# A hybrid block on one core: the last batch's output projection is moved ahead of two other lanes' last products, and its norm reads the bank

## Chip, core and metric

The kernel runs on one core of one Trainium2 chip. The metric is the device time of one execution in microseconds (us), the median of several runs. Engines are named as the profile names them: PE (TensorE matmul), PEld (its weight load), DVE (VectorE), ACT (ScalarE), POOL (GpSimd), SP (the queue that issues most transfers).

## The reference, cut to what matters

Four sublayers, each a residual around a norm without learned factors, on `x` of 4 x 1024 x 128:

```python
x = x + attention(layernorm(x))      # 16 heads, sliding window and stride
x = x + ffn(layernorm(x))
x = x + mamba(layernorm(x))
x = x + ffn(layernorm(x))

def ffn(x):                          # weights are +1 or -1
    h = s0 * conn_dense(k0, concatenate([x, -x]))     # 128 -> 512
    h = s1 * conn_dense(k1, relu(h) * 2)              # 512 -> 512
    return s2 * conn_dense(k2, relu(h) * 2)           # 512 -> 128

def mamba(x):                        # adds its input once more itself
    ...                              # a scan over 1024 steps, 256 channels, 16 states
    y = (scan + u2 * D) * silu(z)
    return x + res_scale * (y @ W_out)
```

The change concerns the very end: the product with `W_out` of the second half of the last batch (512 rows), the norm after it and the MLP (`ffn`) that follows.

## The kernel before, in words

Attention comes first, then a setup of weights, then a long stage in which the scan sets the pace and everything else is slipped between its steps. A "unit" of the scan is one state of one half (512 steps) of one batch: 128 units in all, each with two scans on DVE (`hs`, two halves of 128 channels), one product on DVE (`hc`), one on POOL (`db`), folds on POOL (`hc` pairs) and sums on PE into the bank `pys` (loop at lines 1112 to 1139). When the last state of a part is summed, `gated` (line 1093) multiplies `gate` by `pys` on DVE, once for each half of the channels, and records that the gate is there.

The other work is written as generators that yield a `Piece` before each step (line 598): the engine time it should take, how many PSUM banks it needs, whether it empties a bank. A `Work` (line 625) wraps one generator. While the scan runs, `evictions` and `pieces` (lines 1155 and 1165) issue the next steps of the works in the order of the list `works`, with three banks among them (`SPARE`, line 1142). In this stage the program order on each engine is kept as written (`keep`, line 1240). After the last unit a loop (line 1251) issues, in the order of `works`, whatever is still open, and then the pools of that stage close.

What is still open then belongs to two lanes of MLP work. `pfoc` is the last MLP product of batch 2's second half (512 columns, 16 calls, which appear as 32 PE instructions), `pfob` the second half of the last MLP product of a tile of both batches (16 PE instructions). Each is followed by a residual on DVE (`ox` and `x`) and stores on SP.

Only then, with eight new banks, `mamba_out_own(B - 1)` runs (line 1256, through `weave`, line 640): for each of four groups of 128 rows two calls with the gate and `w_out` and two with an identity that adds the input `xs`; 32 PE instructions into the bank `pmo_own`. ACT copies the bank to `own_x` (`ox`, line 1041). Then the scan's buffers are released (`work.close()`), and two lanes of `late_batch` (line 784) run woven together, each on two of the four groups. Each calls `mlp` (line 682), which

- takes the norm's statistics with `ln_stats` (line 181): `bn_stats` and `bn_aggr` on DVE from `ox`, then four instructions on POOL per lane (add epsilon, power of -1/2, negate the mean, multiply), giving `rs_fc`;
- normalises on ACT, one instruction per group (`fxnc<-ox,rs_fc`);
- transposes on PE (`ftpc`), copies on ACT and subtracts on DVE to get a rounded part and a remainder (`fxnTc`);
- multiplies with the first weights (`pfc`, 16 PE instructions for both lanes), takes rounded part and remainder again on ACT and DVE (`h1c`), multiplies with the second weights (`pgc`, 64), takes the Relu on ACT (`h2c`), multiplies with the third (`pfoc`, 32) and adds the residual on DVE (`ox`), which a store of SP follows.

The trace gives one line, L57, to all compute instructions, that of the helper through which they are issued; they are told apart by tile.

Of the kernel before, what the change touches and what calls it, by code (L numbers as in the profile page):

```python
# [16 lines left out]
F32 = mybir.dt.float32  # L17
# [5 lines left out]
ALU = mybir.AluOpType  # L23
# [3 lines left out]
P = 128  # L27
B, T, C = 4, 1024, 128
# [7 lines left out]
EPS = 1e-5  # L36
# [7 lines left out]
def hybrid_kernel(ctx: ExitStack, tc: tile.TileContext, x, Wq, Wk, Wv, Wo, ln_g, ln_b, W_in, conv_w,  # L44
# [17 lines left out]
    ve, te, sc, gp = (InOrder(e) for e in (nc.vector, nc.tensor, nc.scalar, nc.gpsimd))  # L62
# [118 lines left out]
    def ln_stats(src, name, soon):  # L181

        n = src.shape[1]
        mv = yield from ln_sums(src, name, soon)
        yield Piece(gp=1.7)
        rs = small.tile([P, 2, n], F32, tag="rs", name=f"rs_{name}")
        gp.tensor_scalar_add(rs[:, 0], mv[:, :, 1], EPS)
        gp.tensor_tensor(rs[:, 0], rs[:, 0], minus_half[:, :n], ALU.pow)
        gp.tensor_scalar_mul(rs[:, 1], mv[:, :, 0], -1.0)
        gp.tensor_mul(rs[:, 1], rs[:, 1], rs[:, 0])  # L190
        yield Piece()
        return rs
# [429 lines left out]
    def evict(lump=False, **us):  # L622
        return Piece(evict=True, lump=lump, **us)
# [16 lines left out]
    def weave(*works):  # L640

        while any(w.next for w in works):
            for w in works:
                if w.may():
                    w.run()
# [33 lines left out]

    h1_free = [True]  # L680

    def mlp(u, tiles, split, pool, lane, own=None, soon=False, hasty=False):

        nt = tiles.shape[1]
        cols = nt * C
        parts = 2 if split else 1
        kind = F32R if split else F32

        def wt(w):
            return w if split else w.bitcast(F32)

        def empty(dsts, srcs, relu):


            n = len(srcs)
            yield Piece(n if split else 0, evict=True, sc=0.6 * n, same=soon or hasty)
            for dst, bk in zip(dsts, srcs):
                if relu:  # L700
                    sc.activation(dst[:, 0], bk, AF.Relu)
                else:
                    sc.copy(dst[:, 0], bk)
            if split:
                yield evict(ve=0.7 * n)
                for dst, bk in zip(dsts, srcs):
                    high = dst[:, 0].bitcast(F32)
                    if relu:
                        ve.scalar_tensor_tensor(dst[:, 1], bk, 0.0, high, ALU.max, ALU.subtract)
                    else:  # L710
                        ve.tensor_sub(dst[:, 1], bk, high)

        stats = yield from ln_stats(tiles, f"f{u}", soon)
        yield Piece(sc=1.7)
        xn = fx.tile([P, nt, C], F32, name=f"fxn{u}", tag=f"fxn{lane}", bufs=1)
        ln_apply(xn, tiles, stats[:, 0], stats[:, 1])
        yield fill(1.2)
        tp = bank(f"ftp{u}")[:, :cols]
        for i in range(nt):
            te.transpose(tp[:, i * P : (i + 1) * P], xn[:, i, :], ident)  # L720
        xnT = pool.tile([P, 2, cols], kind, name=f"fxnT{u}", tag=f"fxnT{lane}")
        yield from empty([xnT], [tp], False)
        for f0 in (0, 2):
            yield fill(1.0 if split else 1.8, 2, ready=(lambda: own or h1_free[0]) if f0 == 0 else None)
            if f0 == 0:
                if own:
                    h1 = own(u)
                else:
                    h1 = pool.tile([P, 4, 2, cols], kind, name=f"h1{u}", tag="h1")
                    h1 = [h1[:, f] for f in range(4)]  # L730
                    h1_free[0] = False
                h2 = pool.tile([P, 4, cols], F32, name=f"h2{u}", tag=f"h2{lane}")
            pf = [bank(f"pf{u}_{f0 + f}")[:, :cols] for f in range(2)]
            for f in range(2):
                w = wt(w0[:, (f0 + f) * P : (f0 + f + 1) * P])
                for s in range(parts):
                    te.matmul(pf[f], w, xnT[:, s], start=s == 0, stop=s == parts - 1)
            yield from empty(h1[f0 : f0 + 2], pf, True)
        for f0 in (0, 2):
            yield fill(2.0 if split else 1.8, 2)  # L740
            pg = [bank(f"pg{u}_{f0 + f}")[:, :cols] for f in range(2)]
            for f in range(2):
                for i in range(4):
                    if (i == 0 and f) or (i == 2 and not split):
                        yield more(2.0 if split else 1.8)
                    w = wt(w1[:, i, (f0 + f) * P : (f0 + f + 1) * P])
                    for s in range(parts):
                        te.matmul(pg[f], w, h1[i][:, s], start=i + s == 0, stop=i == 3 and s == parts - 1)
            yield evict(sc=1.2)
            for f in range(2):  # L750
                sc.activation(h2[:, f0 + f], pg[f], AF.Relu)
        if not own:
            h1_free[0] = True
        for i in range(nt):
            if i == 0:
                yield fill(2.0)
                po = bank(f"pfo{u}")[:, :cols]
            elif i == 2:
                yield more(2.0)
            for f in range(4):  # L760
                te.matmul(
                    po[:, i * C : (i + 1) * C], h2[:, f, i * P : (i + 1) * P], w2[:, f].bitcast(F32),
                    start=f == 0, stop=f == 3,
                )
        yield evict(ve=0.75)
        xc = tiles.rearrange("p m c -> p (m c)")
        ve.scalar_tensor_tensor(xc, po, total, xc, ALU.mult, ALU.add)
# [16 lines left out]
    def late_batch(b, groups, *args):  # L784

        yield Piece(ready=lambda: ("o", b, 1) in fed, same=True)
        g = slice(groups[0], groups[-1] + 1)
        tiles = own_x[b][:, g]
        yield from mlp(f"c{b}_{groups[0]}", tiles, True, *args, soon=True)
        nc.sync.dma_start(out[b, T // 2 :].rearrange("(g p) c -> p g c", p=P)[:, g], tiles)  # L790


# [220 lines left out]
            ve.tensor_add(xc, xc, po)  # L1013
        fed.update(("o", *k) for k in pair)

    own_x = {}

    def mamba_out_own(b):

        yield Piece(ready=lambda: ("g", b, 1) in fed, same=True)  # L1020
        gate = mamba_pre[b, 1][0]
        rows = slice((b % 2) * R, (b % 2 + 1) * R)
        own_x[b] = fx.tile([P, 4, C], F32, name=f"ox{b}", tag="mxn", bufs=1)
        yield fill(1.7)
        po = bank(f"pmo{b}_own")
        for g in range(4):
            if g == 2:
                yield more(1.7)
            cols = slice(g * C, (g + 1) * C)
            for h in range(NH):  # L1030
                te.matmul(
                    po[:, cols], gate[:, h, g * P : (g + 1) * P], w_out[:, h], start=h == 0, stop=False,
                    skip_group_check=True,
                )
            for k in range(2):
                te.matmul(
                    po[k * R : (k + 1) * R, cols], ident[rows, rows], xs[b // 2][rows, NT // 2 + 2 * g + k, :],
                    start=False, stop=True, skip_group_check=True,
                )
        yield evict(sc=0.6)  # L1040
        sc.copy(own_x[b].rearrange("p g c -> p (g c)"), po)
        fed.add(("o", b, 1))

# [101 lines left out]
    works = []  # L1145
# [93 lines left out]
    with banks(SPARE), tc.tile_pool(name="wide", bufs=1, space=PSUM) as wide:  # L1239
        keep.append(True)  # L1240
        works.extend([
            first[-1],
            Work(stream(*(mamba_pre_half(*k) for k in parts_in_order[1:]))),
            Work(stream(*(mamba_norm(0, c) for c in second_half), *(mamba_norm(1, c) for c in range(CT)))),
            Work(stream(mamba_out(0, 0), mamba_out(0, 1), mamba_out(1, 0), mamba_out_own(B - 2))),
            *lanes,
        ])
        among_scans[0] = True
        scans(wide, ready)
        among_scans[0] = False  # L1250
        while any(w.next for w in works):
            evictions()
            pieces(forced=True)
        keep.clear()
    with banks(8):
        weave(Work(mamba_out_own(B - 1)))
        work.close()
        with tc.tile_pool(name="ffn_last", bufs=1) as pool:
            def own(u):
                return [pool.tile([P, 2, 2 * C], F32R, name=f"h1{u}_{f}", tag=f"h1{u}_{f}") for f in range(4)]  # L1260

            weave(*(Work(late_batch(B - 1, range(2 * k, 2 * k + 2), pool, k, own)) for k in range(2)))
# [27 lines left out]
```

## Time and profile before

| | |
|---|---|
| median of 3 runs | 929.82 us (927.71 to 930.09) |
| the profiled execution | 926.49 us |
| its span in the profile | 924.7 us |
| mean granted clock of PE | 0.896 |
| attention and setup, until the first scan `hs` | 0 to 324.6 us |
| scans, from the first `hs` to the last `hc` | 324.6 to 885.7 us |
| end of the gate's product on DVE | 890.3 us |
| `pmo_own` on PE | 895.8 to 899.9 us |
| `fxnc`, the last norm, on ACT | 903.05 to 905.5 us |
| `pfc`, `pgc`, last `pfoc` on PE | 906.0 to 921.2 us |
| last residual on DVE | 921.25 to 921.7 us |

The profile tells of one execution. Its chain of waits goes back from the last instruction to whatever released each step; "idle before" names what an engine had waited for. Stretches of time are given with the busy time of an engine, the clock that was granted to TensorE (1.00 is full) and the share of the transfers' engines.

### The profile page before, as it was taken

What the parts mean: (1) busy time and instruction counts of PE and PEld (TensorE: products, weight loads), DVE (VectorE), ACT (ScalarE), POOL (GpSimd) and SP (SyncE); (2) the same over time, 40 slices, a digit from 0 to 9 for tenths busy, and PEclk for the clock granted to TensorE, in tenths of its full rate; (3) what the DMA queues carried; (4) which work ended last, traced back from release to release, by engine and by line L of the source; (5) the groups of instructions that cost most, each with busy time, mean ns of one, the idle gap of its engine ahead of it and who ended that gap; (6) DMA issues with size and microseconds to landing.
All of it is one profiled execution on the core that took longest, in us unless ns stands there. A gap on an engine that the chain in (4) does not pass through costs nothing.

```text
span 924.7 us, 15264 instructions
## 1 busy us (share of the span) xinstructions
PE 759.3 (82%) x5642; PEld 455.5 (49%) x5642; DVE 756.4 (82%) x1013; ACT 592.4 (64%) x1299; POOL 747.9 (81%) x586
## 2 busy tenths in 40 slices
PE   5797768865788979897789798869889798888887
PEld 2455435543466534542356444425446355554566
DVE  6699898999633278889799888898998999999842
ACT  4775537743345577889867767876878765655413
POOL 6699996999533188999989988999989999989621
PEclk9899769997599979897999989968989899898998
DMA  4633123330100111121111122121121212121000
GB/s 122 128 71 70 41 37 68 73 65 2 42 7 1 47 69 50 45 67 70 68 58 58 46 68 71 45 70 46 69 82 62 86 50 78 69 80 58 24 23 12
DMA packets 47162, 53.09 MB, mean 57 GB/s; under 512 B 4824, under 2 KB 38400, under 8 KB 47088
## 3 DMA queue, kind: packets, MB, share of 16 engines
q1 hardware_dynamic: 45920, 51.59, 19.7%
q8 instruction: 44, 0.72, 0.3%
q0 software_dynamic: 608, 0.27, 0.2%
q10 hardware_dynamic: 560, 0.26, 0.1%
q14 instruction: 30, 0.25, 0.1%
HBM read 45.82 MB, written 4.46 MB: 54 GB/s over the span
## 4 chain that ended last, share of the span: by engine, by line
DVE 30%; PE 26%; POOL 17%; ACT 14%; issue 8%; SPq 3%; DMA 1%; DVEq 0%; POOLq 0%; ACTq 0%
DVE hs L57 14%; DVE hc L57 4%; PE pga L57 4%; PE pys L57 4%; POOL db L57 4%; POOL prod L57 3%; DVE S L57 3%; ACT da L57 3%; POOL prodv L57 3%; PE pgb L57 2%; PE pc L57 2%; SPq L330 2%; ACT L57 2%; POOL hc L57 2%; PE pfoa L57 2%
## 5 line engine op out<-in xcount | busy, mean ns | idle before, releaser
L57 POOL TENSOR_TENSOR db<-du,bs 128x1024 f32<-128x1024 f32 x128 | 302.5, 2364 | 0.4 <-DMA bs<-bd 0.4
L57 ACT ACTIVATE da<-dt,a_t 128x512 f32<-128x512 f32 x256 | 175.4, 687 | 126.7 <-DVE hs L57 126.3
L57 POOL TENSOR_TENSOR hc<-hc,hc 128x512 f32<-128x512 f32 x128 | 163.0, 1274 | 43.7 <-DVE hc L57 43.6
L57 DVE TENSOR_TENSOR hc<-hs,pcc 128x1024 f32<-128x1024 f32 x128 | 156.0, 1219 | 28.6 <-PE pcc L57 21.1
L57 DVE TENSOR_TENSOR_SCAN hs<-da,db 128x512 f32<-128x512 f32 x128 | 149.4, 1207 | 14.3 <-ACT da L57 14.1
L57 DVE TENSOR_TENSOR_SCAN hs<-da,carry,db 128x512 f32<-128x512 f32 x128 | 157.1, 1267 | 4.5 <-ACT da L57 4.5
L57 PE MATMUL pys<-hc,ident 128*128 128x512 f32 x256 | 146.0, 655 | 0.8 <-POOL hc L57 0.8
L57 PE MATMUL pcc<-bc,spread 96*128 96x512 bf16 x128 | 52.8, 413 | 34.8 <-DVE hc L57 33.8
L57 PE MATMUL pga<-h1a,w 128*128 128x512 f32 x256 | 73.9, 439 | 3.1 <-ACT gate L57 2.2
L57 PEld LDWEIGHTS pys<-hc,ident 128*128 128x128 f32 x256 | 51.0, 209 | 51.2 <-issue 31.8
L57 POOL TENSOR_TENSOR prodv<-vS,E 128x128 f32<-128x128 f32 (+14 forms) x30 | 69.3, 2311 | 5.8 <-ACT E L57 5.6
L57 POOL TENSOR_TENSOR prod<-kv,qs 128x128 f32<-128x128 f32 (+14 forms) x30 | 71.1, 2369 | 1.5 <-DVE or L57 1.4
L57 PE MATMUL pc<-mxnT,w_conv 128*128 128x512 f32 x128 | 61.7, 608 | 5.9 <-ACT gate L57 5.9
L57 PEld LDWEIGHTS pga<-h1a,w 128*128 128x128 f32 x256 | 51.2, 202 | 27.6 <-issue 7.3
L57 ACT ACT_TABLE_LOAD x48 | 61.6, 1283 | 3.4 <-issue 2.6
L57 PE MATMUL pgb<-h1b,w 128*128 128x512 f32 x192 | 58.9, 453 | 4.4 <-DVE fxnTc L57 3.1
L57 ACT ACTIVATE E<-S 128x512 f32<-128x512 f32 (+15 forms) x62 | 26.5, 473 | 52.3 <-DVE S L57 52.1
L57 PE MATMUL ps<-kx,qT 64*32 64x256 f32 x1008 | 47.8, 448 | 6.3 <-DVE S L57 5.4
L57 PEld LDWEIGHTS pgb<-h1b,w 128*128 128x128 f32 x192 | 38.0, 199 | 26.7 <-issue 7.8
L57 PE MATMUL py<-woT,oT 128*128 128x128 f32 x64 | 18.0, 368 | 40.0 <-ACT oT L57 39.8
L57 POOL TENSOR_TENSOR ep<-ep,eo 128x512 f32<-128x512 f32 x32 | 40.9, 1278 | 9.9 <-ACT ep L57 8.7
L57 ACT COPY ep<-pt 128x512 f32<-128x512 f32 x32 | 18.7, 586 | 38.4 <-DVE eo L57 36.5
(217 smaller groups left out, 1560.9 us busy)
## 6 DMA issues: line engine op xcount, KB each, us to landing
bs<-bd SPq DMA_DIRECT2D x64, 512.0 KB
vr<-vd SPq DMA_DIRECT2D x32, 256.0 KB
vd<-kv SPq DMA_DIRECT2D x8, 256.0 KB
x<-in_L_attn_a_x_dram SPq DMA_DIRECT2D x15, 128.0 KB
kx<-kT SPq DMA_DIRECT2D x104, 16.0 KB
out_dram<-x SPq DMA_DIRECT2D x12, 128.0 KB
taps<-in_L_attn_b_conv_w_dram SPq DMA_DIRECT2D x1, 512.0 KB
k1s<-in_L_ffn_k_dram SPq DMA_DIRECT2D x1, 256.0 KB
```

What stands on the lines that cost most here:

```text
L57: ins = getattr(self.engine, name)(*args, **kwargs)
L330: queues[h % len(queues)].dma_start(kx[rows, :, h % HB, :], kT[rows, :].rearrange("p (t x) -> p t x", t=4))
```

## The change

The projection of the last batch becomes the first of the works that are issued after the last unit, so it stands ahead of `pfoc` and `pfob` on PE and takes one of the three banks of that stage. Its output gets a buffer of its own (`ox_last` instead of `mxn`). For this batch alone the statistics are taken from the PSUM bank `pmo_own`, in front of the copy to `ox`: four `bn_stats`, four `bn_aggr`, then on POOL one add and one power for all four groups, and on DVE one product of negated mean and factor. `mlp` gets these factors and leaves out `ln_stats`; each lane takes its two columns of them. Eight POOL instructions become two.

In the built order of instructions nothing else moves: on PE the block `pmo_own` goes ahead of `pfoc` and `pfob`, on DVE the statistics and the product go ahead of the residuals `ox` and `x`, and ACT keeps its order. The copy to `ox` waits for the four `bn_stats`. The first of the transposes `ftpc` now waits for the residual `x`, for its banks come from the stage that closes there; before, `pmo_own` waited for it.

```diff
-    def mlp(u, tiles, split, pool, lane, own=None, soon=False, hasty=False):
+    def mlp(u, tiles, split, pool, lane, own=None, soon=False, hasty=False, stats=None):
...
-        stats = yield from ln_stats(tiles, f"f{u}", soon)
+        if stats is None:
+            stats = yield from ln_stats(tiles, f"f{u}", soon)
...
-        yield from mlp(f"c{b}_{groups[0]}", tiles, True, *args, soon=True)
+        stats = own_stats[b][:, :, g] if b in own_stats else None
+        yield from mlp(f"c{b}_{groups[0]}", tiles, True, *args, soon=True, stats=stats)
...
-    own_x = {}
+    own_x, own_stats = {}, {}
...
-        own_x[b] = fx.tile([P, 4, C], F32, name=f"ox{b}", tag="mxn", bufs=1)
+        final = b == B - 1
+        own_x[b] = fx.tile([P, 4, C], F32, name=f"ox{b}", tag="ox_last" if final else "mxn", bufs=1)
...
         yield evict(sc=0.6)
+        if final:
+            st = small.tile([P, 4, 6], F32, tag="st", name="st_last")
+            mv = small.tile([P, 4, 2], F32, tag="mv", name="mv_last")
+            for g in range(4):
+                ve.bn_stats(st[:, g], po[:, g * C : (g + 1) * C])
+            for g in range(4):
+                ve.bn_aggr(mv[:, g], st[:, g])
+            rs = own_stats[b] = small.tile([P, 2, 4], F32, tag="rs", name="rs_last")
+            gp.tensor_scalar_add(rs[:, 0], mv[:, :, 1], EPS)
+            gp.tensor_tensor(rs[:, 0], rs[:, 0], minus_half[:, :4], ALU.pow)
+            ve.scalar_tensor_tensor(rs[:, 1], mv[:, :, 0], -1.0, rs[:, 0], ALU.mult, ALU.mult)
         sc.copy(own_x[b].rearrange("p g c -> p (g c)"), po)
...
         among_scans[0] = False
+        works.insert(0, Work(mamba_out_own(B - 1)))
         while any(w.next for w in works):
             evictions()
             pieces(forced=True)
         keep.clear()
     with banks(8):
-        weave(Work(mamba_out_own(B - 1)))
         work.close()
```

## The prediction

> **What bounds the kernel now.** I read the page first, then the chain of waits in order of time for the last 40 us, then the groups by tile of the norm, then TensorE's busy time in short stretches. The page:
>
> ```profile
> span 924.7 us, 15264 instructions
> ...
> PE 759.3 (82%) x5642; PEld 455.5 (49%) x5642; DVE 756.4 (82%) x1013; ACT 592.4 (64%) x1299; POOL 747.9 (81%) x586
> ```
>
> Four engines share the load over the whole span, so no average decides. The built order of instructions and their waits is the same in both kernels until the last product into `pys`, so what the change does lies after 889.6 us, in the last 35 us. There the chain reads (start, length, what):
>
> ```profile
> 889.59 3.57 PE pfoc L57 x32
> 893.16 1.80 PE pfob L57 x16
> 894.96 0.02 issue
> 894.99 0.76 DVE x L57
> 895.75 0.04 issue
> 895.79 4.12 PE pmo_own L57 x32
> ...
> 904.63 0.50 ACT fxnc L57
> 905.13 0.04 issue
> 905.17 0.86 PE ftpc L57 x2
> 906.04 3.82 PE pfc L57 x16
> 909.86 7.79 PE pgc L57 x64
> 917.64 3.58 PE pfoc L57 x32
> ```
>
> TensorE first finishes the last products of the two other lanes (`pfoc` of batch 2, `pfob`, 5.4 us), waits 0.83 for VectorE's residual that frees the banks, projects the last batch (`pmo_own`), idles for the norm, and then runs the last MLP, where it alone sets the end. The gate that `pmo_own` needs is ready at 890.32 (its second half starts at 889.63 and takes 0.69), so the block waits 5.5 us for others' work. The second fact is the clock. In stretches of 3.41 us (columns: PE busy and count, granted clock, DMA share, GB/s):
>
> ```profile
> 893.36:896.77 3.41, 2.56 (x23) 1.00 0.25 77
> 896.77:900.19 3.42, 3.12 (x26) 1.00 0.33 77
> 900.19:903.60 3.41, 0.00 (x1) 1.00 0.00 0
> 903.60:907.01 3.41, 2.69 (x8) 0.50 0.00 0
> 907.01:910.43 3.42, 3.42 (x18) 0.50 0.02 5
> 910.43:913.84 3.41, 3.41 (x31) 1.00 0.00 0
> ```
>
> The 3.7 us in which TensorE waits for the norm (899.9 to 903.6) halve its clock until 910.43. The 16 matmuls of `pfc` take 3.82 us, 239 ns each; the 64 of `pgc`, of the same 256 columns and nearly all after the recovery, take 122 ns each.
>
> [...] clock changes fall on one 3.41 us grid. Over the whole span, 28 stretches at full clock were followed by half clock; 26 of these were at most 56% busy, two were 62% and 89%, and most above 60% kept it. [...] ScalarE's copy of the bank has to wait for VectorE's four statistics; no run yet shows its time. [...] The trace has no statistics from a bank.
>
> **The change part by part**, on the profiled execution's own clock (span 924.7, whole execution 926.49, so 1.8 us lie around it; the median of the runs, 929.82, is 3.3 above this execution).
>
> 1. `pmo_own` ahead of the lanes' products. In the new order the first matmul waits for the gate's first half and for a bank whose last reader ended before 888. The second waits for the gate's second half, 890.32 + 0.04. The first gate half's share of the block, about 0.3 of its 4.12, can be done by then, so the block ends at 890.36 + 3.8 = 894.2 (before: 899.9). TensorE idles 0.75 here that it did not.
>
> 2. `pfoc` and `pfob` follow: 894.2 + 3.57 + 1.80 = 899.6. Their residuals on VectorE and three output stores on SP's queue move 4.6 us later, the last store's issue to about 901.7. The two final stores are next on that queue and are asked for only about 913 to 915, so cover is 11 us. The handover of the banks, 0.83, now stands between `pfob` and the transposes instead: transposes may start at 900.4.
>
> 3. The norm, beside 2. From the tiles' groups:
>
> ```profile
> L57 DVE BATCH_NORM_STATS2 st_fc<-ox x8: 259/264/294, 842.6 to 901.3; 128x6 f32<-128x128 f32 x8
> L57 POOL TENSOR_TENSOR rs_fc<-rs_fc,minus_half x3: 722/727/1036, 847.1 to 903.6; 128x2 f32<-128x2 f32 x2, 128x4 f32<-128x4 f32 x1
> ```
>
> Removed: the copy (0.59) ahead of the statistics, and eight POOL instructions in two lanes, 901.51 to 904.59, 3.1 us. Added: four statistics from the bank, 0.25 each back to back on SBUF in the chain[...]; I take 0.28, 1.1 in sum, bounds 0.9 to 1.4. Four aggregates at 0.17, of which 0.5 to 0.7 shows. POOL: 0.23 for the sum with epsilon, 1.04 for the power of four columns, 0.16 for two handovers. VectorE's product of mean and factor, 128x4, has no row; 0.08 plus 0.1 to 0.25, by the 0.17 of an aggregate. From 894.25 this reaches 895.4, 896.0, 897.4, 897.65. The copy runs at 895.4 to 896.0 under it. ScalarE normalises four columns of tiles: 0.49 + 3 x 0.39 = 1.65, the first pair ready at 898.5, all at 899.3. The transposes can't start before 900.4, so the norm has 1.1 us of slack for all and 1.9 for the first pair; what it costs beyond that would be paid in full. The added wait on VectorE (for POOL's power) has the residual of `pfoc` (input ready 897.8) queued behind it, and that of `pfob` (899.6), which frees the banks: 0.2 and 2.0 us of slack.
>
> 4. Transposes to first product: 0.81 before for the last pair (905.17 to 905.98). At full clock the first pair takes some 0.35, ScalarE's copy 0.35 and a handover: 0.8. `pfc` starts at 901.2 instead of 905.98: 4.8 us.
>
> 5. The clock. TensorE's idle time falls from one piece of 3.7 us to 0.8 and a few tenths. In the worst stretch of 3.41 us about 1.1 is idle, 68% busy, on the side that kept the clock. So `pfc` takes 16 x 0.122 = 1.95 and 0.1 of waits, ending 903.2 instead of 909.86: 6.6. But its evictions were hidden under the slow clock: ScalarE takes eight in 2.73 (0.34 each), starting about 902.1, VectorE its eight to 905.3. By the new order the fifth `pgc` matmul needs ScalarE's fifth, 903.8, against 903.6; the tenth needs its seventh. I count 0.4 of stalls. `pgc` itself had about 0.6 us at half clock and gains 0.3: it ends at 903.2 + 7.5 + 0.4 = 911.1 instead of 917.64. The last `pfoc`, residual and store are as before.
>
> Sum: 6.5 us, of which 4.8 come from the order with the shorter norm and 1.7 from the clock. Profiled execution: span 918.2, execution 920.0. On the median: 929.82 - 6.5 = 923.3.
>
> **The rivals.** (a) The clock is halved all the same: 68% is above most of the stretches that lost it, yet 62% and 89% did once each. Then only the 4.8 stays, less a few tenths where the half clock lasts longer: 925.1. (b) The norm ends last: statistics from a bank at twice the SBUF row (+1.1) and the unseen product at 1 us (+0.8) use up the 1.1 of slack and put `pfc` 0.8 late: a gain of 5.7, 924.1. For it speaks that no row shows these two operations; against it the 1.1 us of slack. (c) The block does not really move, because its bank is freed later than the listed wait suggests: then only the norm is shorter. From the block's end to the last factor it took 4.7 us (899.9 to 904.6) and would take 3.4 by the terms of 3, but four normalisations follow in a row (1.65) where two did (0.88): a gain of 0.5, 929.3. The waits in the built order speak against it. (d) Slower: VectorE's statistics are slowed by reading a bank while TensorE writes its neighbours. TensorE writes all through them now and did not before. VectorE's queue stands behind them with both residuals, and the bank handover behind these. It decides once a statistic takes over 1.75 us instead of 0.28 (4.8 of start and 1.1 of slack in four): `pfc` then starts after 905.98 with the same cold clock. At 2.7 us each, 9.7 more, less the slack of 1.1, the last MLP starts 8.6 late against my 901.2, and with the cold clock the time is 929.82 + 3.8 = 933.6. Against it: VectorE's gate and residual rows read banks beside a writing TensorE all through the scans at 0.66 to 0.75 for 512 columns.
>
> **How the numbers follow.** Forecast 0.82, (a) 0.08, (b) 0.05, (c) 0.03, (d) 0.02. The three runs of before spread over 2.4 us, so a median may stand 1 to 1.5 off by chance; the unknown costs add 0.7, and where on the 3.41 us grid a run's recovery falls (908.6 to 912 us, by when the busy stretch begins) moves the clock's part by 0.8 either way. Together: 921.0 to 925.9, which takes in (a) and (b). A measurement of this kernel can tell about 0.3%, 2.8 us, from no change. The forecast, (a) and (b) lie beyond it by 2 us or more: faster 0.92 after scatter; within it (c) and scatter: 0.05; slower 0.03.
>
> **What would show it.** In the new profile: `pmo_own` starting near 889.6 and pausing for the gate; the transposes released by VectorE's residual `x`, not by ScalarE's `fxnc`; `pfc` at about 120 ns per matmul with the clock at 1.00; ScalarE, not TensorE, releasing the first `pgc`. Wrong, if the transposes wait for `fxnc`, if the clock reads 0.50 after 900 us, or if anything before 889 us has moved.

## The result and the profile after

| | before | after |
|---|---|---|
| median of six runs | 928.5 us (925.27 to 930.09) | 920.37 us (918.48 to 923.73) |
| the profiled execution | 926.49 us | 918.99 us |
| its span in the profile | 924.7 us | 917.2 us |
| mean granted clock of PE | 0.896 | 0.901 |

The ratio of the times is recorded as 0.9924 (it is not the quotient of the two medians, 0.9912), with a 95% interval of 0.9904 to 0.9945: 5 to 9 us faster. The page of the changed kernel, to be laid beside the one shown of before:

```profile
span 917.2 us, 15260 instructions
...
PE 753.5 (82%) x5642; PEld 450.8 (49%) x5642; DVE 756.8 (83%) x1014; ACT 592.3 (65%) x1299; POOL 747.2 (81%) x580
```

The counts tell what was built: six instructions fewer on POOL, one more on DVE (the product); TensorE has the same 5642. Its busy time fell by 5.8 us, from 759.3 to 753.5, with the same work. Of this, 2.5 us lie in the last stage (26.35 to 23.83 us from the last product into `pys` to the last `pfoc`); the other 3.3 lie ahead of it, where the two kernels do the same, and are not the change's.

The chain of waits in order of time (start, length, what):

```profile
885.80 2.59 PE pys L57 x6
...
888.41 0.70 DVE gate L57
...
889.15 3.88 PE pmo_own L57 x30
893.03 3.77 PE pfoc L57 x32
896.80 1.80 PE pfob L57 x16
...
898.62 0.76 DVE x L57
899.38 0.14 issue
899.52 0.42 PE ftpc L57 x2
...
899.96 0.38 ACT fxnTc L57
...
900.39 2.19 PE pfc L57 x16
902.58 7.56 PE pgc L57 x64
910.13 3.58 PE pfoc L57 x32
```

POOL, which held the chain for 3 us before, and ScalarE's copy and `fxnc` are gone from it. What stands between `pfob` and the last MLP is the residual `x`, then two transposes and the copy `fxnTc`. The busy time of the engines over the same place, in stretches laid on the clock's own grid (columns: PE, PEld, DVE, ACT, POOL busy and count, granted clock, DMA share, GB/s):

```profile
895.66:899.08 3.42, 2.92 (x27) 2.73 (x25) 1.37 (x3) 1.65 (x4) 0.02 (x1) 1.00 0.14 44
899.08:902.49 3.41, 2.73 (x21) 2.52 (x22) 1.80 (x6) 1.82 (x7) 0.00 (x0) 1.00 0.45 115
```

Before, one of these stretches was empty and the next two ran at half clock. Now the handover (898.60 to 899.52) is cut by a boundary at 899.08, TensorE is busy 86% and 80% of the two stretches, and the clock stays at 1.00 to the end of the last `pfoc`.

One measure is used from here on: the **tail**, from the end of the last product into `pys` to the end of the last `pfoc`, both read in the chain. Before: 889.59 to 921.22, 31.6 us. After: 888.39 to 913.71, 25.3 us. So the change saved 6.3 us there. The other 1.2 us of the 7.5 by which the two spans differ lie ahead of 889, where the two kernels hold the same instructions in the same order; they are not the change's. In the twelve profiles of this case the end of `pys` stood anywhere from 886.9 to 892.9 us, with that same work ahead of it, so a single span tells little and the tail much.

The tail's place on the grid, however, is the same in all twelve. The clock last rises on the scan's side at 861.53 in the kernel after, which a stretch of a tenth of a microsecond shows by its mean clock (0.84, so 0.68 of it at full):

```profile
861.50:861.60 0.10, 0.10 (x2) 0.03 (x1) 0.10 (x1) 0.10 (x1) 0.10 (x1) 0.84 0.00 0
```

`pys` ends 26.9 us later. Found in the same way, that distance is 26.85 to 26.97 us in every profile, before and all experiments included. The grid's steps are 3.41 us, so each kernel enters the tail 0.3 to 0.5 us ahead of a boundary, and its gaps fall on the same parts of the grid each time; the two profiles of the changed kernel agree in this.

### The profile page after: what moved, and what is told of

Same layout as the page of the kernel before. It is cut to its first block, busy times and chain, and to the rows that moved or that the text cites. A ratio compares the mean times of both kernels' runs of the same rounds, so it can differ in the third digit from the quotient of the medians.

```text
span 917.2 us, 15260 instructions
## 1 busy us (share of the span) xinstructions
PE 753.5 (82%) x5642; PEld 450.8 (49%) x5642; DVE 756.8 (83%) x1014; ACT 592.3 (65%) x1299; POOL 747.2 (81%) x580
## 4 chain that ended last, share of the span: by engine, by line
DVE 32%; PE 26%; POOL 20%; ACT 12%; issue 8%; DMA 2%; SPq 0%; DVEq 0%; POOLq 0%; ACTq 0%
DVE hs L57 14%; POOL db L57 5%; DVE hc L57 5%; PE pga L57 4%; DVE S L57 4%; PE pys L57 4%; POOL prod L57 3%; POOL hc L57 3%; POOL prodv L57 3%; PE pc L57 3%; ACT da L57 2%; ACT L57 2%; PE pgb L57 2%; PE pfoa L57 2%; DVE or L57 2%
```

## Experiments

The ratios are to the kernel before, run on the same chip as each, and are given as recorded; they are not quotients of medians. "Start of `pfc`" is counted from the end of `pys`, and it, the time of `pfc` and the tail come from one profile of each kernel. The edits of the two kernels named "before, ..." are shown against the kernel before, all others against the changed kernel; where two edits stand under one heading, the second is added to the first.

| kernel | median, us | ratio to before | start of `pfc` | `pfc` takes | tail |
|---|---|---|---|---|---|
| before (four sets of runs) | 926.29 to 928.5 | | +16.4 | 3.82 | 31.6 |
| after | 920.37 | 0.9924 [0.9904, 0.9945] | +12.0 | 2.19 | 25.3 |
| order only | 920.50 | 0.9934 [0.9909, 0.9958] | +12.0 | 2.19 | 25.3 |
| norm only | 927.20 | 1.0005 [0.9990, 1.0019] | +15.5 | 3.82 | 31.1 |
| before, 28 matmuls in the gap | 925.47 | 0.9995 [0.9976, 1.0014] | +16.4 | 3.15 | 31.3 |
| before, 44 matmuls in the gap | 924.02 | 0.9976 [0.9959, 0.9993] | +16.4 | 2.27 | 29.8 |
| after, norm 1.9 us longer | 919.77 | 0.9931 [0.9908, 0.9954] | +12.0 | 2.18 | 25.3 |
| after once more | 919.16 | 0.9916 [0.9894, 0.9939] | +12.0 | 2.18 | 25.3 |
| after, norm 5.6 us longer | 926.04 | 0.9994 [0.9981, 1.0007] | +15.5 | 3.79 | 31.2 |
| the same with 36 matmuls | 923.32 | 0.9962 [0.9950, 0.9974] | +15.3 | 2.18 | 28.6 |
| after, `pfob` first | 918.98 | 0.9920 [0.9894, 0.9946] | +11.2 | 2.18 | 24.6 |
| after, statistics behind the residuals | 928.57 | 1.0010 [0.9994, 1.0027] | +16.0 | 3.82 | 31.4 |

The theory: moving the block pays, by 4.4 us of earlier start and 1.9 us of clock. The rivals: the shorter norm pays; or the clock has no share and the second part comes from elsewhere.

### The order alone

The block is moved, but the norm is that of before (copy first, statistics of the copy, eight POOL instructions).

```diff
         yield evict(sc=0.6)
-        if final:
-            st = small.tile([P, 4, 6], F32, tag="st", name="st_last")
...
-            ve.scalar_tensor_tensor(rs[:, 1], mv[:, :, 0], -1.0, rs[:, 0], ALU.mult, ALU.mult)
         sc.copy(own_x[b].rearrange("p g c -> p (g c)"), po)
```

> The projection moved ahead, the norm left as it was (copy first, statistics of the copy, eight POOL instructions in two lanes). Theory (the order pays, the norm now lies under the two other lanes' products): from the block's end at 893.0 us, the old norm needs 4.7 us to the last factor and 0.9 for the last pair, 898.6, and the transposes may not start before 899.5. So pfc starts where it does in the changed kernel, with the full clock, and the gain over before is the whole 7 to 8 us (ratio 0.992). Rival (the shorter norm carries part of it): the transposes wait for fxnc and 1.3 to 2 us of the gain are lost (ratio 0.994).

Measured: the tail is 25.3 us, the same as with the whole change. The timeline of this kernel (start, length, engine, instructions; in brackets the idle time ahead and what ended it):

```profile
896.27 0.88 ACT L57 ACTIVATE fxnc<-ox,rs_fc 128x128 f32<-128x128 f32 x2 [0.70 <-POOL rs_fc L57]
897.16 0.75 DVE L57 SCALAR_TENSOR_TENSOR x<-pfob,total,x 128x512 f32<-128x512 f32 x1 [1.04 <-PE pfob L57]
898.05 0.63 PE L57 MATMUL ftpc<-ident,fxnc 128*128 128x128 f32 x4 [0.94 <-DVE x L57]
```

The old norm's last `fxnc` ends at 897.15, 0.9 us ahead of the transposes, which wait for the residual `x`. Once the block is early, even the long norm is covered. The new norm bought nothing here but more slack. The ratio, 0.9934, lies between what the theory (0.992) and the rival (0.994) expected, with an interval that holds both; it is the chain that decides between them.

### The norm alone

Statistics from the bank and joint factors, the block where it was.

```diff
-        works.insert(0, Work(mamba_out_own(B - 1)))
...
     with banks(8):
+        weave(Work(mamba_out_own(B - 1)))
         work.close()
```

> The norm from the bank with the factors of both lanes together, the projection left behind the lanes' products. Theory: the factors come 1.3 us earlier, but four normalisations then follow in a row where two did, so pfc starts about 0.5 us earlier, and TensorE still idles over 3 us, so its clock is still halved: a gain of 0.5 us (ratio 0.9995). Rival (the norm is what counts): 1.3 us or more and no half clock, 3 us (ratio 0.997).

Measured: no difference in the runs, 0.5 us in the tail. The end of this kernel's chain of waits:

```profile
901.97 0.49 ACT fxnc L57
...
902.50 1.25 PE ftpc L57 x3
903.75 3.82 PE pfc L57 x16
907.57 8.25 PE pgc L57 x64
```

From the end of `pmo_own` to the first transpose in the chain it now takes 3.9 us (898.6 to 902.50) instead of 5.3 (899.9 to 905.17), but the transposes take 1.25 instead of 0.86, and `pgc` 8.25 instead of 7.79. TensorE still idles, its clock still halves (0.50 from 905.4 to 908.8), and of the 1.0 us by which the work starts earlier (0.5 was expected), 0.5 goes to more work at half clock. This and the run before it refute the rival that the norm pays.

### Filling the gap of the kernel before

The clock's share by itself: the kernel before, with matmuls that nobody reads, into a bank of their own, behind `pmo_own`. Fourteen calls, 28 instructions:

```diff
         weave(Work(mamba_out_own(B - 1)))
+        busy = bank("busy")
+        for i in range(14):
+            te.matmul(busy[:, :C], mamba_pre[B - 1, 1][0][:, 0, :P], w_out[:, 0], start=True, stop=True)
```

> The kernel before, with 28 more matmuls (14 calls of 128 columns, about 3.2 us, into a bank that nobody reads) while TensorE waits for the norm. The output is the same. Theory (the idle piece costs the clock): the clock stays at 1.00 after 900 us, pfc takes 2.2 us instead of 3.8, and the kernel gets 1.9 us faster by doing more work (ratio 0.998). Rival (the clock falls for another reason, or the evictions bound pfc anyway): no gain or a loss of some tenths.

Measured: 0.3 us in the tail, nothing in the runs. Busy time in stretches of this kernel's grid:

```profile
901.96:905.37 3.41, 2.33 (x12) 1.50 (x13) 0.85 (x2) 1.83 (x6) 0.87 (x3) 1.00 0.00 0
905.37:908.78 3.41, 3.41 (x19) 3.41 (x18) 2.75 (x8) 2.48 (x8) 0.00 (x0) 0.50 0.00 0
```

The filler ended at 901.5. The four transposes came in pairs at 901.9 and 903.5 with idle time between them, which left a stretch 68% busy, and half clock followed it, one stretch of it instead of two and later, so that it hit the end of `pfc` and the start of `pgc`. As a test of the clock's share this run is inconclusive: it moved the slow stretch instead of removing it. In this place 68% busy was not enough. The share of busy time is no rule by itself, though. In the kernel before, a stretch with 89% lost the full clock and one with 42% kept it (columns: PE busy and count, granted clock, DMA share, GB/s):

```profile
418.91:422.32 3.41, 3.04 (x7) 1.00 0.00 0
422.32:425.74 3.42, 2.29 (x3) 0.50 0.49 152
...
449.63:453.04 3.41, 1.42 (x7) 1.00 0.01 4
453.04:456.46 3.42, 2.56 (x10) 1.00 0.40 150
```

With the traces of before and after each laid on its own grid, all 14 stretches at full clock that were 65 to 70% busy, to the nearest per cent, kept it. Of those above 60% four lost it (62 and 89% before, 62 and 73% after), each with 6 or 7 PE instructions, but 18 with 7 or fewer kept it. What the clock goes by beside the recorded busy time stays open.

### The same filler, longer

Twenty-two calls (44 instructions) instead of fourteen.

> As the first filler run on the kernel before, but 44 more matmuls (22 calls, about 4.9 us), so that TensorE is busy until the transposes: the shorter filler left 2.4 us of idle time behind it, and the clock was halved there for 3.4 us. Theory (idle time costs the clock): 1.00 until the end, pfc takes 2.2 us, and from the last product into pys to the last pfoc it is 29.7 us instead of 31.6, 1.9 us faster (ratio 0.998) though pfc starts no earlier. Rival: the clock is halved all the same, 31.6.

Measured: a ratio of 0.9976, its interval below 1, and a tail 1.8 us shorter. The chain of this kernel:

```profile
904.80 0.33 PE ftpc L57
...
905.22 2.27 PE pfc L57 x16
907.49 7.56 PE pgc L57 x64
```

`pfc` starts at +16.4 us as before, since nothing on the path to it has changed, and takes 2.27 instead of 3.82. So 44 added matmuls make the kernel faster, through the clock alone. The size, 1.8, is near the clock's share in the change, 1.9.

### Slack of the norm: 1.9 us more

Six additions of zero on POOL between the epsilon and the power, 0.23 us each and 0.07 between them.

```diff
             gp.tensor_scalar_add(rs[:, 0], mv[:, :, 1], EPS)
+            for _ in range(6):
+                gp.tensor_scalar_add(rs[:, 0], rs[:, 0], 0.0)
             gp.tensor_tensor(rs[:, 0], rs[:, 0], minus_half[:, :4], ALU.pow)
```

> The changed kernel with six more POOL additions of zero in the norm's chain, 0.31 us each with the handover, 1.9 us in all. Theory (about 1.9 us of slack for the last pair, 2.7 for the first): the factors come at 897.7 instead of 895.8, the last pair is normalised at 899.5, just when the transposes may start, and the time stays within 0.2 us of the changed kernel's (ratio to before 0.992 to 0.993). Rival (the norm is on the path): 1.9 us slower (0.9945).

Measured: tail 25.3, unchanged. The chain shows that the slack is just used up:

```profile
898.47 0.78 ACT fxnc L57 x2
...
899.33 0.42 PE ftpc L57 x2
...
900.20 2.18 PE pfc L57 x16
```

`fxnc` has now come into the chain, and yet `ftpc` starts 11.1 us after `pys`, exactly as without the additions (888.39 to 899.52).

### The changed kernel once more

No edit; it ran beside the three kernels that follow.

> The changed kernel itself beside the next three, on one chip. A ratio to before of 0.990 to 0.9945, as measured first.

Measured: 0.9916 and a tail of 25.3 us to the tenth, with `pys` ending at 888.85 instead of 888.39. The tail repeats; what is ahead of it moves.

### Norm 5.6 us longer, with and without a filler

First eighteen additions in place of six.

> The changed kernel with eighteen more POOL additions of zero in the norm's chain, 5.6 us. Theory: the slack is used up, VectorE's two residuals stand behind the product of the factors (at 901.3) and free the banks at about 903.1, so pfc starts near 904.0, 3.6 us later than in the changed kernel; TensorE idles over 4 us, its clock is halved, and pfc and the first of pgc lose 1.5 to 2.5 us more: 5 to 6 us slower than the changed kernel, about 2 us faster than before (ratio 0.997 to 0.999). Rival (the clock does not fall with idle time): 3.6 us slower only (0.996).

Then the same kernel, with 18 calls (36 instructions) of the matmul above issued behind `pfob`:

```diff
+        def filler():
+            yield Piece(ready=lambda: not any(w.next for w in works[:-1]), same=True)
...
+            for i in range(18):
+                te.matmul(busy[:, :C], mamba_pre[B - 1, 1][0][:, 0, :P], w_out[:, 0], start=True, stop=True)
+        works.append(Work(filler()))
```

> As the run before it, with 36 more matmuls (18 calls of 128 columns, 4.0 us, into a bank that nobody reads) behind the lanes' products, while TensorE waits for the lengthened norm. Theory: pfc starts at the same place, 904.0, but at full clock, and the time is 1.5 to 2.5 us shorter than without the filler. Rival: the same time.

Measured, the first: all of the gain is gone (0.9994, tail 31.2). Its chain:

```profile
903.21 0.40 DVE x L57
903.60 0.40 ACT fxnc L57
...
904.10 1.09 PE ftpc L57 x4
905.22 3.79 PE pfc L57 x16
```

The 5.6 us less some 2.0 of slack come out as a start 3.5 us later. The other 2.4 of the 5.9 us that the tail grew go with the clock, as the stretches show:

```profile
900.30:904.20 3.90, 0.10 (x1) 0.14 (x2) 1.48 (x3) 1.48 (x4) 1.80 (x5) 0.94 0.00 0
904.20:907.60 3.40, 3.37 (x15) 2.96 (x16) 1.34 (x4) 1.63 (x6) 0.00 (x0) 0.50 0.60 159
```

The two terms came out as expected (3.6 and 1.5 to 2.5 us). That 2 us of gain over before would be left did not: it was reckoned from the 8 us between the first medians, of which only 6.3 belong to the tail.

Measured, the second: `pfc` starts at nearly the same place, and takes 2.18:

```profile
903.68 0.43 PE ftpc L57 x2
...
904.55 2.18 PE pfc L57 x16
```

The tail is 28.6, 2.6 us shorter than with the gap open. The two intervals, 0.9981 to 1.0007 and 0.9950 to 0.9974, don't meet. The pair separates the two terms of the sum: late start 3.3 us (28.6 against 25.3), clock 2.6.

### `pfob` first

The wait for the gate, 0.31 us of idle TensorE and half-used time around it, might be filled: `pfob` ahead of the projection.

```diff
-        works.insert(0, Work(mamba_out_own(B - 1)))
+        works.remove(lanes[1])
+        works[:0] = [lanes[1], Work(mamba_out_own(B - 1))]
```

> The changed kernel with the one product of lane 1 that is still open (pfob, 1.8 us on TensorE) put ahead of the projection, under the 0.7 us in which TensorE waits for the gate. Theory: the block starts 1.1 us later, its norm still fits (all four tiles normalised at 898.7), pfoc ends at 897.9 instead of 898.6, and the residual that frees the banks is now that of pfoc: 0.6 to 0.7 us faster than the changed kernel (ratio to before about 0.0007 lower). Rival: the norm, now 1.1 us later, ends last and eats it: no gain.

Measured: the tail is 24.6, 0.7 us below the change. The timeline of this kernel:

```profile
901.43 1.65 ACT L57 ACTIVATE fxnc<-ox,rs_last 128x128 f32<-128x128 f32 x4 [1.33 <-DVE rs_last L57]
902.29 0.75 DVE L57 SCALAR_TENSOR_TENSOR ox<-pfoc,total,ox 128x512 f32<-128x512 f32 x1 [0.96 <-PE pfoc L57]
903.19 0.63 PE L57 MATMUL ftpc<-ident,fxnc 128*128 128x128 f32 x4 [0.94 <-ACT fxnc L57]
```

The products of TensorE end 9.4 us after `pys` instead of 10.2, and the whole handover now lies in one stretch of the grid, which is 73% busy and keeps the clock:

```profile
900.04:903.45 3.41, 2.48 (x23) 2.31 (x23) 0.91 (x2) 1.70 (x5) 1.04 (x1) 1.00 0.00 0
```

The last normalisation (903.08) and the residual that frees the banks (903.04) now end together: the order is balanced. In this order the short norm should matter, by an estimate of 1.0 us: the old one ended 10.2 us after `pys` in the kernel with the order alone (897.15), the new one 9.2 in the changed kernel (897.62). No run has this order with the old norm. On the whole time the new order shows as 918.98 against 919.16 us for the changed kernel beside it. The intervals overlap almost wholly, so that it is the better kernel is read from one profile each and not from the times.

### The projection early, its statistics behind the residuals

TensorE's order as in the change; DVE's statistics, the copy and the factors wait until both residuals are issued.

```diff
+        if final:
+            yield Piece(ready=lambda: not any(w.next for w in works[1:]), same=True)
         yield evict(sc=0.6)
```

> The changed kernel, the projection still ahead on TensorE, but its statistics, copy and factors issued after the two lanes' residuals, so that VectorE reaches them last. Theory (the gain is the overlap of the norm with the lanes' products, not the place of the projection by itself): statistics start at 11.0 us after the last product into pys instead of 4.7, the last pair is normalised at 15.6, TensorE idles over 4 us, the clock is halved, and the whole gain is gone: 31.5 us from that product to the last pfoc, as in the kernel before (ratio 1.000). Rival (the place on TensorE alone pays): at least half of the gain stays (0.996).

Measured: nothing is left (1.0010, tail 31.4). The timeline of this kernel:

```profile
902.89 0.75 DVE L57 SCALAR_TENSOR_TENSOR x<-pfob,total,x 128x512 f32<-128x512 f32 x1 [1.03 <-PE pfob L57]
903.56 0.88 DVE L57 BATCH_NORM_STATS2 st_last<-pmo_own 128x6 f32<-128x128 f32 x4
906.99 1.63 PE L57 MATMUL ftpc<-ident,fxnc 128*128 128x128 f32 x4 [4.14 <-ACT fxnc L57]
```

An early projection is worth nothing by itself: TensorE has done it all and then idles 4.1 us for the norm, as before. What pays is that DVE, POOL and ACT do the norm while TensorE multiplies for the other lanes.

## Why the prediction was right, step by step

The forecast was 923.3 us with a range of 921.0 to 925.9, the likeliest case being 6.5 us less than before. The runs gave 920.37, just under the range's lower end; the tail gave 6.3 us. The mechanism is the one forecast, and its size was right within 0.2 us. The median missed for a reason that is no part of the mechanism: the base was high. Three more runs brought the median of before from 929.82 to 928.5, and in the three later sets, of 27, 38 and 27 runs, it was 927.17, 926.29 and 927.14. From 927 a gain of 6.3 us leads to 920.7, where 920.37 was measured. The range allowed 1 to 1.5 us for that and 0.8 for the place of the tail on the clock's grid; the first was too little, and the second wasn't needed, since that place didn't vary (26.85 to 26.97 us behind the last rise).

1. **`pmo_own` ahead.** Right. The block ended 4.64 us after `pys` (forecast 4.6). Two of its matmuls ran with the gate's first half, then TensorE idled 0.31 us for the second half. The forecast's 0.75 of idle time was the whole wait for the gate; it left out the 0.3 us of matmuls that its own sum had put there.
2. **`pfoc` and `pfob` follow.** Right to 0.2 us: their end was 10.2 after `pys`, forecast 10.0. The handover of the banks, forecast at 0.83, took 0.92 (898.60 to 899.52), as 0.14 instead of 0.04 went by behind the residual. The stores never came into the chain.
3. **The norm beside them.** Right in kind, too dear in size. From the groups of the changed kernel (minimum, median, maximum ns, first and last start):

```profile
L57 DVE BATCH_NORM_STATS2 st_last<-pmo_own x4: 281/282/299, 893.1 to 893.7; 128x6 f32<-128x128 f32 x4
L57 POOL TENSOR_TENSOR rs_last<-rs_last,minus_half x1: 1037/1037/1037, 894.6 to 894.6; 128x4 f32<-128x4 f32 x1
L57 DVE SCALAR_TENSOR_TENSOR rs_last<-mv_last,rs_last x1: 161/161/161, 895.7 to 895.7; 128x4 f32<-128x4 f32 x1
```

   Four statistics took 0.89 us from first start to last end (forecast 1.1, by the author's estimate of 0.28 each; lower bound 0.9). ScalarE's copy of the bank began at 894.05, behind the last of them (893.97). The unseen product took 0.16 (0.1 to 0.25). The factors were there 7.5 us after `pys` (forecast 8.06), all four normalisations at 897.62, so the slack was 1.9 us and not 1.1:

```profile
895.97 1.65 ACT L57 ACTIVATE fxnc<-ox,rs_last 128x128 f32<-128x128 f32 x4 [1.33 <-DVE rs_last L57]
899.52 0.63 PE L57 MATMUL ftpc<-ident,fxnc 128*128 128x128 f32 x4 [0.94 <-DVE x L57]
```

   The run with 1.9 us more confirms it: nothing lost, and nothing left over. For the reading "the price of each part of the norm doesn't matter while it is covered" the run with the order alone is the proof.
4. **Transposes to `pfc`.** 0.87 against 0.8. The start of `pfc` came out 12.0 us after `pys`, forecast 11.6: the 0.4 is 0.2 from step 2, 0.1 from the handover and 0.1 from here. So the order gave 4.4 and not 4.8 us.
5. **The clock.** Right in size, on a ground that is a likelihood and no rule. The clock stayed at 1.00 to the end of the tail, `pfc` took 2.19 us (forecast 2.05), and from the start of `pfc` to the end of the tail it took 13.3 instead of 15.2 us, a gain of 1.9 (forecast 1.7). The fillers show this term apart from the order, at 1.8 and 2.6 us. But the forecast put the worst stretch at 68% busy and said that this is on the side that keeps the clock. A stretch with 68% lost it in the kernel with 28 matmuls, though all 14 of 65 to 70% in the traces of before and after kept it. In the change no stretch was as empty, since a boundary cuts its gap and leaves 86% and 80%; that the cut saved the clock is likely, but not shown. The trace of before would have told where the boundaries lie, had I laid the new order on them. One more term was mis-sized: 0.4 us of stalls for `h1c` evictions did not come. `pgc` follows `pfc` in the chain without a gap, in 7.56 us; ScalarE emptied its eight tiles in 2.32 us, not 2.73. The sign "ScalarE releasing the first `pgc`" was therefore not seen.

The rivals: (a) the clock halved anyway: it stayed in all five profiles that had the block early and the norm covered, in one of them (`pfob` first) with the gap whole in one stretch, 73% busy. Laid in the middle of a stretch (897.19 to 900.60), the gap of the change would leave 65%, 2.23 of 3.41 us; whether the clock stays then, no run tried. (b) The norm ends last: not in the change, but the run with 5.6 us more shows that it happens as priced once the slack is gone, with the clock's loss on top, which the rival's 924.1 left out since it assumed under a microsecond of delay. (c) Only the norm is shorter: the tail of that run is 0.5 us shorter, as forecast, but by another sum: 1.0 from the start, less 0.5 to the clock. The forecast had no term for the clock there and came right by chance. (d) Statistics slowed by reading a bank beside a writing TensorE: 281 to 299 ns with TensorE busy all through, where 1.75 us were needed; refuted.

Open: why the same instructions ahead of the tail end up to 6 us apart from one profile to the next while they keep their distance to the clock's last rise within 0.12 us. The scatter arises before that rise; where the work falls into step with the grid wasn't looked for.

## What to carry to other kernels

Where the last stage waits for a chain of small steps on other engines, put the product that feeds this chain ahead of independent products on TensorE, and put the chain's own steps ahead of these products' evictions on their queues; the first without the second gained nothing here (an early projection with late statistics gave 1.0010). Once the chain is covered, making it shorter is worth nothing (a tail of 25.3 us with the old norm and with the new), so measure its slack before rewriting it. And price an idle gap of TensorE twice: by its length, and, where the clock falls behind it, by the matmuls that run at half clock: here, by the fillers, 1.8 and 2.6 us behind gaps of 3.7 and 4.2. Behind the change's gap of 0.9 us it stayed at 1.00.

## What the runs showed of the hardware that was not expected

- Matmuls whose product nobody reads made the kernels here faster: 44 in the gap of the kernel before took 1.8 us off the tail, 36 in the lengthened one 2.6. Both fillers reached to the transposes (TensorE busy for all of 899.0 to 904.0 in the first, for 3.51 of the 3.70 us to 903.7 in the second); 28 matmuls, which ended at 901.5 with 1.3 us of idle time still to come (0.39 and 0.87), were too few.
- The clock changed on a grid with steps of 3.41 us, and a stretch of it need not be idle to lose the clock: one with 68% busy lost it and one with 73% kept it at the end of these kernels, and elsewhere one with 89% lost it and one with 42% kept it.
- The place of the tail on the grid was not a matter of chance: in twelve profiles the tail began 26.85 to 26.97 us after a rise of the clock, though its time from the start varied by 6 us.
- Statistics from the bank were not seen to be dearer than those from SBUF: 281 to 299 ns (median 282) from the bank, 259 to 294 (median 264) from `ox`, and 260 to 295 (median 285) from `x` at the start of the kernel before.
- POOL's power took 0.72 us for two columns and 1.04 for four, so one joint instruction cost less than two (1.44). The whole shorter norm gave 0.5 us of the tail where it was on the path (the norm alone) and nothing where it was covered (25.3 us with it and without it).
